# Four attention layers on 128 small graphs: graphs in pairs, three Strassen projections, leaky relu in PSUM, a planner by due times

## The chip, the cores and the metric

The kernel runs on one NeuronCore of a Trainium2 chip. The core has a matrix engine (TensorE, PE in the profile, with its weight loads as PEld), a vector engine (VectorE, DVE), an activation engine (ScalarE, ACT), a general engine (GpSimd, POOL), a queue engine that here issues nearly all transfers (SyncE, SP), and 16 DMA engines. Each engine works through its own list of instructions in order[...]. TensorE writes to PSUM[...]; GpSimd and DMA work on SBUF. The metric is the time of one execution on the device, in microseconds.

## The reference

128 graphs of 128 nodes with 512 features go through four attention layers. Each layer's result is added to its input and layer-normed.

```python
x = _layernorm(x + _L0_gnn_ref(x, adj, ...))   # scores from x itself, mixes x
x = _layernorm(x + _L1_gnn_ref(adj, x, ...))   # two GAT layers: 512 -> 4 heads x 256, elu, then 1024 -> 512, one head
x = _layernorm(x + _L2_gnn_ref(x, adj, ...))   # 8 heads of 64
x = _layernorm(x + _L3_gnn_ref(x, adj, ...))   # scores from 32 features, mixes x, elu
```

An attention is always the same: two numbers per node and head, their outer sum through a leaky relu with slope 0.2, a mask from the adjacency matrix, a softmax, and a product with the features:

```python
h = jnp.einsum('bnf,hfo->bhno', x, W)
e = jax.nn.leaky_relu(s1[..., :, None] + s2[..., None, :], negative_slope=ALPHA)
attn = jax.nn.softmax(jnp.where(mask, e, NEG_INF), axis=-1)
h_prime = jnp.einsum('bhnm,bhmo->bhno', attn, h)
```

There are 15 attention heads per graph: one, four, one (both parts of the second layer), eight and one. All arithmetic is f32.

## The kernel before

One graph is one stage of a software pipeline. A function `graph(g)` writes down the graph's operations as a list of `Op` objects, each with its engine, a cost in us, the buffers that it reads and writes, and a closure that emits it.

Order. `Pipeline.plan` places one graph's operations on a circle of 28 us (`PERIOD`), each engine's spans disjoint modulo the period, with a random shift from a fixed seed. `Pipeline.order` then takes all graphs' operations by those times and runs a list schedule over them, with 8 PSUM banks and a counted number of buffers for each size, and may take an operation up to 20 us (`AHEAD`) out of turn. The result is one fixed list per engine. The planner knows costs and latencies[...].

A graph's way. `first` loads x and adj, makes masks (`mask`, L738), two scores by a product with a running sum (`score`, L744), and calls `spread` and `attend`. `spread` (L580) brings a column of scores to every partition: a transpose on VectorE (L589), a transfer to a row in DRAM (L592), a transfer that broadcasts it (L596). `attend` (L637) has for each head of 128 x 128: the leaky relu on ScalarE from that broadcast with the own score as bias (L646, SBUF to SBUF), the mask with a running minimum on VectorE (L654, two SBUF inputs), the exponential with its sum on ScalarE (L663), and a reciprocal (L671). `turned` (L602) transposes through DRAM: 32x32 blocks on VectorE (L607), a transfer out (L612) and a transfer back in pieces (L622, or L617 where the result is a moving operand). `mixed` (L722) is the product, `resid` (L732) adds, `norm` (L678) is the layer norm: statistics on VectorE, a root on ScalarE (L685, L686), an offset on GpSimd (L692), the scaling on ScalarE (L699).

Three projections. The first (`project`, L704) multiplies x of one graph by `w1s` in 4 column blocks of 258 columns and 4 steps over the features: 16 matmuls per graph, each block in its own bank, copied out by ScalarE (L717). The second (`halves`, L749) takes two graphs together as a 2x2 block matrix and does Strassen's scheme (the variant of Winograd): 7 products instead of 8, of 4 matmuls with 257 columns each, 28 for a pair; sums of the left side on GpSimd (L780), partial results copied by ScalarE (L807) and added by VectorE (L812). The third (`project` again, with `wha`) has 2 blocks of 273 columns and 4 steps, 8 matmuls per graph.

`third` also holds the last layer: `scores` and `normed` do small arithmetic on two numbers per node on VectorE (L956 to L969). Each working buffer is a tile of its own; tiles of equal size share places.

SyncE issues 30 transfers per graph, 60 for two. The part of `attend` that matters most:

```python
nc.scalar.activation(z.ap[:, h, :], db.ap[:, h0 + h, :], AF.Prelu, bias=src(h0 + h), alpha=SLOPE)
nc.vector.tensor_tensor_reduce(
    out=zz.ap[:, h, :]..., in0=z.ap[:, h, :]..., in1=mask.ap..., scale=-1.0, scalar=FMAX,
    op0=ALU.add, op1=ALU.min, accum_out=nm.ap[:, h : h + 1])
```

Of the kernel before, what the change touches and what calls it, by code (L numbers as in the profile page):

```python
# [26 lines left out]

PERIOD = 28.0
LATENCY = {"PE": (0.0, 0.8), "DVE": (0.15, 1.44), "ACT": (0.1, 1.44), "POOL": (0.1, 1.44), "SP": (7.06, 7.06)}
FLOW = {"PE": (0.0, 0.6), "DVE": (0.15, 0.8), "ACT": (0.1, 0.8), "POOL": (0.1, 0.8), "SP": (4.5, 4.5)}
AHEAD = 20.0
URGENCY = 0.6
BANKS = 8

SEED, SPREAD = 989, 8.0


class Buf:


    def __init__(self, tag, shape, dtype=F32):
        self.tag, self.shape, self.dtype = tag, shape, dtype
        self.size = 1
        for d in shape[1:]:
            self.size *= d

        if dtype is F32 and shape[0] == P and self.size in (P, 4 * P, 8 * P) and not tag.startswith(("ps", "scr")):  # L50
            self.tag = f"w{self.size}"
        self.ap = self.slot = None

    def view(self, tl):
        if self.tag[0] == "w" and len(self.shape) > 2:
            dims = "abc"[: len(self.shape) - 1]
            tl = tl.rearrange(f"p ({' '.join(dims)}) -> p {' '.join(dims)}", **dict(zip(dims, self.shape[1:])))
        return tl


class Op:
    def __init__(self, engine, cost, emit, ins, outs, extra, uses=(), dma=0.0):
        self.dma = dma
        self.engine, self.cost, self.emit, self.extra = engine, cost, emit, extra
        self.wait = 0
        self.ins, self.outs = ins, outs
        self.uses = list(uses)
        self.bufs = list(dict.fromkeys([*ins, *outs, *uses]))

    def done(self, reader=None):  # L70
        own, other = LATENCY[self.engine]
        return self.cost + self.extra + (own if reader is self.engine else other)


class Pipeline:
    def __init__(self, make, n, place):
        self.make, self.n, self.place = make, n, place

    def plan(self, ops):


        before, after = [set() for _ in ops], [[] for _ in ops]
        last, readers = {}, {}
        for k, op in enumerate(ops):
            for b in op.ins:
                before[k].add(last[b])
            for b in op.outs:
                if b in last:
                    before[k].add(last[b])
                before[k].update(readers.get(b, ()))  # L90
            before[k].discard(k)
            for q in before[k]:
                after[q].append(k)
            for b in op.ins:
                readers.setdefault(b, set()).add(k)
            for b in op.outs:
                last[b], readers[b] = k, set()
        left = [0.0] * len(ops)
        for k in reversed(range(len(ops))):
            left[k] = ops[k].cost + max(  # L100
                (left[q] + ops[k].done(ops[q].engine) - ops[k].cost for q in after[k]), default=0.0
            )
        taken = {e: [] for e in LATENCY}
        times, ready, missing = [0.0] * len(ops), [0.0] * len(ops), [len(q) for q in before]
        waiting = [k for k in range(len(ops)) if not missing[k]]
        rng = random.Random(SEED)
        shift = [SPREAD * rng.random() for _ in ops]
        while waiting:
            k = min(waiting, key=lambda k: (ready[k] - URGENCY * left[k] + shift[k], k))
            waiting.remove(k)  # L110
            op, t = ops[k], ready[k]
            spans = taken[op.engine]
            while True:
                u = t % PERIOD
                clash = [
                    y + d - u for x, y in spans for d in (-PERIOD, 0.0, PERIOD)
                    if u < y + d - 1e-9 and x + d < u + op.cost - 1e-9
                ]
                if not clash:
                    break  # L120
                t += min(clash) + 1e-9
                assert t < ready[k] + 2 * PERIOD, "the period is too short"
            spans.append((t % PERIOD, t % PERIOD + op.cost))
            times[k] = t
            for q in after[k]:
                ready[q] = max(ready[q], t + op.done(ops[q].engine) + max(ops[q].wait, 0) * PERIOD)
                missing[q] -= 1
                if not missing[q]:
                    waiting.append(q)
        return times  # L130

    def run(self, setup):
        times, events = self.plan(self.make(None)), [(t, -1, k, op) for k, (t, op) in enumerate(setup)]
        for g in range(self.n):
            for k, op in enumerate(self.make(g)):
                if op is not None:
                    events.append((g * PERIOD + times[k], g, k, op))
        events.sort(key=lambda e: e[:3])
        for g, op in self.order(events):
            for b in op.outs:  # L140
                if b.ap is None and b.slot is not None:
                    b.ap = self.place(b, g)
            op.emit()

    def order(self, events):

        ops, n = [e[3] for e in events], len(events)
        ends, first, last, readers, open_uses = {}, {}, {}, {}, {}
        before, after = [0] * n, [[] for _ in ops]
        makes, coming = [[] for _ in ops], {}  # L150
        for i, op in enumerate(ops):
            need = {last[b] for b in op.ins + op.uses if b in last}
            for b in op.outs:
                need.update([last[b]] if b in last else [], readers.get(b, ()))
                if b not in first:
                    first[b] = events[i][0]
                    if b.tag != "const":
                        makes[i].append(b)
                        coming.setdefault(b.tag, []).append(i)
            need.discard(i)  # L160
            before[i] = len(need)
            for q in need:
                after[q].append(i)
            for b in op.ins + op.uses:
                readers.setdefault(b, []).append(i)
            for b in op.outs:
                last[b], readers[b] = i, []
            for b in op.bufs:
                open_uses[b] = open_uses.get(b, 0) + 1
                ends[b] = max(ends.get(b, 0.0), events[i][0] + op.done())  # L170

        free = {}
        for b, t in first.items():
            if b.tag != "const":
                places = free.setdefault(b.tag, [])
                s = next((s for s, e in enumerate(places) if e <= t), len(places))
                places[s : s + 1] = [ends[b]]
        assert len(free["ps"]) <= BANKS, "too few banks"
        free = {tag: [(0.0, s) for s in range(BANKS if tag == "ps" else len(p))] for tag, p in free.items()}
        ready, released, clock, lane = [0.0] * n, {}, {e: 0.0 for e in FLOW}, 0.0  # L180
        known = {e: [i for i in range(n) if not before[i] and ops[i].engine == e] for e in FLOW}
        issued, low, out = [False] * n, 0, []

        def start(i):
            t = max(clock[ops[i].engine], ready[i])
            for b in makes[i]:

                rank = 0
                for q in coming[b.tag]:
                    if q >= i or rank >= len(free[b.tag]):  # L190
                        break
                    rank += 1
                if rank >= len(free[b.tag]):
                    return None
                t = max(t, free[b.tag][rank][0])
            return t

        while len(out) < n:
            best = None
            for e, waiting in known.items():  # L200
                found = None
                for i in waiting:
                    if events[i][0] > events[low][0] + AHEAD and i != low:
                        break
                    t = start(i)
                    if t is not None and (found is None or t < found[0]):
                        found = (t, i)
                        if t <= clock[e]:
                            break
# [34 lines left out]
def tile_gat_stack(  # L244
# [63 lines left out]
    def mark():  # L308

        return Buf("const", [P, 1])  # L310
# [740 lines left out]
```

## Time and profile before

| what | us |
|---|---|
| median of 3 runs | 3246.22 (3245.11 to 3246.83) |
| span of the profiled execution | 3258.4 |
| first output leaves (from the span's start) | 355.1 |
| last input is loaded | 2996.0 |
| mean granted clock of TensorE | 0.976 of full |

The profile is of one execution, whose span is 12 us (0.4%) above the median of the runs. A row of the groups has the line, the engine, the operation, output and inputs, shapes and count, then the busy time together and the mean of one in ns, then the idle time of the engine just before these instructions and who ended it. A busy time is the time in which at least one instruction of the group ran, so where instructions overlap in the pipeline it is less than count times mean. DMA carries 606 MB with 1.66 million packets, 1.31 million of them under 512 bytes; the 16 DMA engines are busy 75% of the span.

### The profile page before, as it was taken

The page shows a single profiled execution, that of the slowest core. Times are in us where ns is not written, and L with a number is a line of the kernel's source. Part 1 is how long each engine was busy: PE and PEld are TensorE (multiplying, and loading weights), DVE is VectorE, ACT ScalarE, POOL GpSimd, SP SyncE. Part 2 cuts the span into 40 slices and gives each one's busy share as a digit, 9 for nine tenths or more (in the row PEclk, how much of TensorE's full clock was granted, in tenths as well). Part 3 has the DMA queues.
Part 4 walks back from the last instruction along what each step waited for, and adds up shares of the span by engine and source line. Part 5 has one row for each costly group of instructions (what it writes and reads, how often), then busy time and mean ns, then how long its engine had stood idle before and what let it go on. Part 6 is the DMA issues. An engine that isn't in the chain of part 4 may idle for free. (4 is left out here: it accounts for less than half of the span.)

```text
span 3258.4 us, 62058 instructions
## 1 busy us (share of the span) xinstructions
PE 3066.8 (94%) x14822; PEld 2488.7 (76%) x14822; DVE 2779.0 (85%) x9833; ACT 2451.2 (75%) x8741; POOL 1895.1 (58%) x2347
## 2 busy tenths in 40 slices
PE   6899999999999999999999999999999999999984
PEld 4688887787777877877777778777787777878853
DVE  4779888888888988898888889889898898989875
ACT  2457787787777777787777877777877777778875
POOL 4655655665565655665555665565566556565533
PEclk7899999999999999999999999999999999999985
DMA  4358777877877877877778777877787787777875
GB/s 119 94 136 196 183 205 188 200 193 190 203 187 188 205 186 192 201 190 200 188 187 200 191 188 204 189 190 201 191 204 187 188 205 188 196 196 190 197 174 129
DMA packets 1657567, 606.08 MB, mean 186 GB/s; under 512 B 1311562, under 2 KB 1508170, under 8 KB 1657204
## 3 DMA queue, kind: packets, MB, share of 16 engines
q1 hardware_dynamic: 1655836, 598.97, 75.0%
q8 instruction: 120, 1.97, 0.2%
q14 instruction: 243, 1.99, 0.2%
q0 software_dynamic: 576, 2.10, 0.2%
q10 hardware_dynamic: 792, 1.06, 0.1%
HBM read 374.43 MB, written 227.48 MB: 185 GB/s over the span
## 5 line engine op out<-in xcount | busy, mean ns | idle before, releaser
L710 PE MATMUL ps<-w1s,w 128*128 128x258 f32 x4096 | 926.9, 384 | 48.5 <-DMA w<-scr 25.0
L710 PEld LDWEIGHTS ps<-w1s,w 128*128 128x128 f32 x4096 | 777.0, 191 | 186.3 <-DVE xl L812 39.5
L654 DVE CUSTOM_DVE_ANT_0 w<-w,w 128x128 f32<-128x128 f32 x1920 | 861.1, 544 | 65.6 <-ACT w L646 49.2
L794 PE MATMUL ps<-w2s,w 128*128 128x257 f32 x3584 | 849.0, 383 | 8.5 <-POOL w L780 8.4
L663 ACT ACTIVATE w<-w,nm 128x128 f32<-128x128 f32 x1920 | 748.0, 394 | 98.2 <-DVE nm L654 76.3
L794 PEld LDWEIGHTS ps<-w2s,w 128*128 128x128 f32 x3584 | 669.1, 191 | 188.8 <-issue 80.0
L646 ACT ACTIVATE w<-w,xl 128x128 f32<-128x128 f32 x1536 | 488.8, 389 | 279.9 <-DMA w<-row 259.1
L607 DVE STREAM_TRANSPOSE w<-w 128x512 f32<-128x512 f32 (+1 forms) x1024 | 551.5, 540 | 34.3 <-ACT w L663 13.3
L710 PE MATMUL ps<-wha,w 128*128 128x273 f32 x2048 | 502.3, 398 | 7.3 <-DMA w<-scr 6.9
L710 PEld LDWEIGHTS ps<-wha,w 128*128 128x128 f32 x2048 | 383.2, 192 | 87.4 <-DVE w L607 6.3
L699 ACT ACTIVATE w<-w,mr,rd 128x512 f32<-128x512 f32 x512 | 415.2, 811 | 33.9 <-POOL mr L692 33.0
L692 POOL TENSOR_SCALAR mr<-mv,rd 128x1 f32<-128x1 f32 x512 | 160.1, 313 | 409.4 <-ACT rd L686 201.8
L663 ACT ACTIVATION_READ_ACCUMULATOR w<-w,nm 128x1 f32 x1920 | 368.1, 192 | 0.0
L681 DVE BATCH_NORM_STATS2 st<-w 128x6 f32<-128x512 f32 x512 | 337.2, 668 | 5.4 <-POOL w L986 4.6
L881 POOL TENSOR_TENSOR xl<-xl,b1t 128x512 f32<-128x512 f32 x256 | 335.2, 1310 | 1.6
L938 PEld LDWEIGHTS ps<-xl,w 128*128 128x128 f32 x2048 | 274.3, 196 | 80.8 <-issue 24.4
L646 ACT ACTIVATE w<-w,sc 128x128 f32<-128x128 f32 x384 | 152.3, 397 | 227.6 <-DMA w<-row 226.6
L725 PE MATMUL ps<-w,w 128*128 128x512 f32 x512 | 277.4, 624 | 32.6 <-DMA w<-scr 31.6
L738 POOL TENSOR_SCALAR w<-adj 128x128 f32<-128x128 int32 x256 | 192.4, 752 | 188.2 <-DMA adj<-in_adj_dram 75.1
L717 ACT COPY xl<-ps 128x258 f32<-128x258 f32 (+1 forms) x768 | 273.2, 362 | 31.8 <-PE ps L710 31.3
L938 PE MATMUL ps<-xl,w 128*128 128x66 f32 x2048 | 265.2, 273 | 27.7 <-DMA w<-scr 14.4
L654 DVE DVE_READ_ACCUMULATOR2_ANT nm<- 128x1 f32 x1920 | 290.5, 151 | 0.0
(213 smaller groups left out, 4258.8 us busy)
## 6 DMA issues: line engine op xcount, KB each, us to landing
scr<-w SPq DMA_DIRECT2D x640, 256.0 KB
w<-scr SPq DMA_DIRECT2D x640, 256.0 KB
w<-row SPq DMA_DIRECT2D x128, 512.0 KB
w<-in_x_dram SPq DMA_DIRECT2D x128, 256.0 KB
w<-row SPq DMA_DIRECT2D x128, 256.0 KB
out_dram<-w SPq DMA_DIRECT2D x128, 256.0 KB
w<-row SPq DMA_DIRECT2D x384, 64.0 KB
scr<-w SPq DMA_DIRECT2D x384, 64.0 KB
```

Of the source, the lines that this page charges most:

```text
L607: op("DVE", 0.12 + 0.133 * n, lambda: nc.vector.transpose(zb.ap.rearrange("p b h c -> p h b c"), src.ap.rearrange("p (h b c) -> p h b c", ...
L646: nc.scalar.activation(z.ap[:, h, :], db.ap[:, h0 + h, :], AF.Prelu, bias=src(h0 + h), alpha=SLOPE)
L654: nc.vector.tensor_tensor_reduce(out=zz.ap[:, h, :].rearrange("p (b a) -> p a b", b=4), in0=z.ap[:, h, :].rearrange("p (a b) -> p a b", b= ...
L663: nc.scalar.activation(zz.ap[:, h, :], zz.ap[:, h, :], AF.Exp, bias=nm.ap[:, h : h + 1], scale=-1.0, accum_out=rs.ap[:, h : h + 1],)
L681: op("DVE", 0.6, lambda: nc.vector.bn_stats(st.ap, y.ap), [y], [st])
L699: op("ACT", 0.7, lambda: nc.scalar.activation(y.ap, y.ap, AF.Identity, bias=mr.ap, scale=rd.ap), [y, rd, mr], [y])
L710: op("PE", w * 4 / 2400 + 0.006, lambda k=k: nc.tensor.matmul(px.ap[:, :w], lhsT=lhs.ap[:, k, :], rhs=wa(k, c), start=(k == 0), stop=(k == ...
L717: op("ACT", 0.06 + w / 1200, lambda: nc.scalar.copy(dst(), px.ap[:, :w]), [px], [t])
L725: op("PE", width * 4 / 2400, lambda: nc.tensor.matmul(pa.ap[:, :width] if len(xv.shape) == 2 else pa.ap.rearrange("p (s c) -> p s c", s=2) ...
L794: return lambda: nc.tensor.matmul(q[b].ap[:, :C2], lhsT=x()[:, k, :], rhs=w2s[:, slot, k, :], start=(fresh and k == 0), stop=(k == 3), ski ...
L881: op("POOL", 1.3, lambda nh=nh: nc.gpsimd.tensor_add(xl.ap[:, nh, : 2 * FH], xl.ap[:, nh, : 2 * FH], b1t[:, nh * 2 * FH : (nh + 1) * 2 * F ...
L938: op("PE", 0.225, lambda u=u, h=h: nc.tensor.matmul(pa.ap[:, u * CH : (u + 1) * CH], lhsT=pt.ap[:, u, :], rhs=xl3.ap[:, h * CH : (h + 1) * ...
```

## The change

Two graphs now are one unit of the pipeline, `pair(n)`; there are 64.

1. Transfers. `first` loads x and adj of both graphs with one transfer each, the output leaves with one, and `spread` and `turned` carry both graphs' data in one transfer where they can. SyncE issues 31 transfers per pair. The bytes are the same.
2. Projections. All three go through `strassen`, which takes the two graphs as a 2x2 block matrix. The first is done for each half of the columns: 2 x 7 products of 2 matmuls with 258 columns; the second 7 of 4 with 257; the third 7 of 2 with 273. `w1s` and the third weights (`w3s`, formerly `wha`) get three more combined blocks, made once by four subtractions on VectorE (`combined`). `sums` makes four sums of the left side on GpSimd for each projection. One product uses three banks; at most two products are open at once (`PRODUCTS`).
3. `attend` writes the leaky relu to a PSUM bank, from which the mask reads. Up to four heads share a bank.
4. `norm` handles both graphs' small numbers in one instruction each; the arithmetic of `scores` and `normed` on two numbers per node goes to GpSimd except for one reduction.
5. Order. `plan` walks one pair's operations from the end and gives each a due time: 1.28 (`STRETCH`) times the longest way before it. Pair n is due 44.5 us (`PACE`) after pair n-1. `lay_out` runs one list schedule over everything, by due times, up to 80 us ahead. It books [...]the time of DMA descriptors, and the parts of an operation, so that the second head's mask may follow the second head's relu. The setup's due times move forward, for the third weights from 70..134 to 45..77.
6. Memory. All working tiles of at least 64 f32 per partition are parts of one tile, `arena`, at places found from their lifetimes in that schedule.

```diff
-PERIOD = 28.0
-AHEAD = 20.0
-SEED, SPREAD = 989, 8.0
+STRETCH, PACE, AHEAD = 1.28, 44.5, 80.0
+SEED, SPREAD = 1, 0.0
+BANKS, PRODUCTS = 8, 2
+LOADS = 15.0
...
+    def combined(t, w, ready, engines):
...
+        sub(0, engines[0], 5, 2, 3, ready)
+        sub(1, engines[1], 3, 3, 0, [*ready, marks[0]])
+        sub(2, engines[2], 4, 2, 3, [marks[1]])
+        sub(3, engines[3], 6, 1, 4, [marks[2]])
+        return marks
...
-    w1s = const.tile([P, 4, 2, N1], F32, name="w1s")
+    w1s = const.tile([P, 7, 2, N1], F32, name="w1s")
...
     def attend(db, h0, nh, src, mask, scaled=False):
-            z, zz, nm, rs, ri = (Buf(f"{t}{nh}", s) for t, s in (
+        z = bank()
+        zz, nm, rs, ri = (Buf(f"{t}{nh}", s) for t, s in (
...
-                        z.ap[:, h, :], db.ap[:, h0 + h, :], AF.Prelu, bias=src(h0 + h), alpha=SLOPE
+                    z.ap[:, h * P : (h + 1) * P], db.ap[:, h0 + h, :], AF.Prelu, bias=src[1]()[:, h : h + 1], alpha=SLOPE
...
-            op("ACT", 0.08 + 0.293 * nh, prelu, [db, src.buf], [z])
-            op("DVE", 0.08 + 0.225 * nh, masked, [z, mask], [zz, nm])
-            op("ACT", 0.39 * nh, exp, [zz, nm], [zz, rs])
+        op("ACT", [0.4] * nh, prelu, [db, src[0]], [z])
+        op("DVE", [0.24] * nh, masked, [z, mask[0]], [zz, nm])
+        op("ACT", [0.387] * nh, exp, [zz, nm], [zz, rs])
...
+        def root():
+            nc.scalar.activation(rd.ap, mv.ap[:, :, 1], AF.Ln, bias=eps)
+            nc.scalar.activation(rd.ap, rd.ap, AF.Exp, scale=-0.5)
...
+    def sums(left, shape):
...
+        (a11, a12), (a21, a22) = left
+        summed(0, ALU.add, a21, a22)
+        summed(1, ALU.subtract, own[0], a11)
+        summed(2, ALU.subtract, a11, a21)
+        summed(3, ALU.subtract, a12, own[1])
...
+    def strassen(left, s, w, nk, wide, cols, to, out, ready):
+        pa, pb, pc = bank(), bank(), bank()
...
+        product(pa, left[0][0], 0, True)
...
+        taken(pa, t1)
+        product(pc, left[0][1], 1, True)
+        added(pc, t1, 0, 0)
+        product(pa, s[1], 4, False)
+        product(pb, s[0], 3, True)
+        taken(pa, u2)
+        taken(pb, v)
+        product(pa, s[2], 5, False)
+        product(pb, s[3], 2, False)
+        added(pa, v, 1, 1)
+        added(pb, u2, 0, 1)
+        product(pa, left[1][1], 6, False)
+        copied(pa, wide, lambda: to(1, 0), joins=[out[1]])
...
+        def normed():
+            nc.gpsimd.tensor_add(sc4.ap, sc4.ap, sz.ap)
+            nc.gpsimd.tensor_mul(sc4.ap, sc4.ap, rd.ap.unsqueeze(2).to_broadcast([P, 2, 2]))
+            nc.gpsimd.tensor_mul(sw.ap, swf.ap.unsqueeze(1).to_broadcast([P, 2, 2]), md.ap.unsqueeze(2).to_broadcast([P, 2, 2]))
+            nc.gpsimd.tensor_add(sc4.ap, sc4.ap, sw.ap)
...
+    for n in range(pairs):
+        begin = len(ops)
+        pair(n)
+        if offsets is None:
+            own = ops[begin:]
+            offsets = plan(own)
+        for o, t in zip(ops[begin:], offsets):
+            o.due = n * PACE + t
```

`taken` copies a bank to SBUF on ScalarE; `added` adds a bank and such a copy on VectorE; `product` is a chain of matmuls into a bank, where a last argument False adds to what the bank holds.

## The prediction

> **What bounds the kernel now.** I read the page's shares first, then the table by stages, then the groups of TensorE and VectorE in an undisturbed stretch, then the waits.
>
> ```profile
> PE 3066.8 (94%) x14822; PEld 2488.7 (76%) x14822; DVE 2779.0 (85%) x9833; ACT 2451.2 (75%) x8741; POOL 1895.1 (58%) x2347
> ...
> PE   6899999999999999999999999999999999999984
> ```
>
> TensorE is nearly full in all slices but the first two and the last. Stages (columns: PE, weight loads, DVE, ACT, POOL busy, each with its instructions, then the granted clock, the DMA share and GB/s):
>
> ```profile
> 0.00:100.00 100.00, 73.47 (x207) 45.56 (x208) 52.14 (x173) 30.91 (x90) 53.83 (x61) 0.80 0.42 112
> ...
> 1000.00:2000.00 1000.00, 964.13 (x4747) 788.44 (x4748) 876.91 (x3136) 782.74 (x2813) 597.29 (x741) 1.00 0.79 193
> ...
> 3100.00:3200.00 100.00, 77.63 (x300) 57.91 (x299) 76.98 (x299) 75.68 (x270) 34.36 (x56) 0.80 0.76 183
> ```
>
> ```profile
> L710 PE MATMUL ps<-w1s,w 128*128 128x258 f32 x1312 | 295.5, 383 | 18.2 <-DMA w<-scr 9.7 <-DVE st L681 3.1 <-DVE ri L671 3.0
> L794 PE MATMUL ps<-w2s,w 128*128 128x257 f32 x1170 | 276.2, 382 | 0.6 <-POOL w L780 0.6
> L710 PE MATMUL ps<-wha,w 128*128 128x273 f32 x656 | 158.0, 393 | 0.0
> ```
>
> These are the groups from 1000 to 2000 us. An f32 matmul leaves two records. A graph needs 16 matmuls of w1s, so 32 records, and 1312 records are 41.0 graphs in 1000 us: 24.39 us a graph, 48.78 us a pair. TensorE is busy 964.13/20.5 = 47.03 us of a pair and idle 1.75. So in steady state TensorE bounds. 128 graphs at 24.39 are 3122 us; filling and draining cost the other 136 us of the 3258.4. Per pair the others are busy: DVE 42.8, ACT 38.2, POOL 29.1 us, and DMA 0.79 x 48.78 = 38.5 us.
>
> Part of DVE's time is not work. Two engines at the same moment (start, duration):
>
> ```profile
> 1001.87 0.37 DVE L654 CUSTOM_DVE_ANT_0 w<-w,w 128x128 f32<-128x128 f32 x1
> ...
> 1002.09 1.50 DVE L654 CUSTOM_DVE_ANT_0 w<-w,w 128x128 f32<-128x128 f32 x1
> ```
>
> ```profile
> 1002.07 1.27 POOL L780 TENSOR_TENSOR w<-w,w 128x512 f32<-128x512 f32 x1
> ```
>
> The same masking instruction takes 0.37 us alone and 1.50 us when a GpSimd sum began 0.02 us earlier; it ends 0.25 us after that sum.
>
> ```profile
> L654 DVE CUSTOM_DVE_ANT_0 w<-w,w 128x128 f32<-128x128 f32 x620 | 274.6, 539 | 19.2 <-ACT w L646 12.5 <-DMA row<-w 5.3 <-ACT w L663 0.7
> ...
> L812 DVE TENSOR_TENSOR xl<-ps,u 128x257 f32<-128x257 f32 x81 | 32.6, 403 | 9.0 <-ACT u L807 8.9
> ...
> L959 DVE TENSOR_TENSOR sc<-sc,xl 128x2 f32<-128x2 f32 x41 | 26.6, 648 | 1.4
> ```
>
> Its mean is 539 ns; the line's own answer for 1000 to 1500 us gives a median of 383. L812, one input in PSUM, lies between 378 and 427 ns throughout. L959, two tiny inputs in SBUF, takes 648.
>
> [...]
>
> **The change, part by part, per pair of graphs.**
>
> TensorE. The first projection goes from 32 matmuls of 258 columns to 28, the third from 16 of 273 to 14. From the groups: 295.5/656 = 0.450 us and 158.0/328 = 0.482 us each, so 4 x 0.450 + 2 x 0.482 = 2.77 us. The groups overlap: all of TensorE's groups add to 1036 us against 964 busy, so I take 0.93 of it, 2.6 us. The second projection keeps its 28, the attention products keep count and shape. Busy 47.0 - 2.6 = 44.4 us.
>
> DVE. 30 masks lose the lock: 30 x (0.539 - 0.383) = -4.7. [...] I take +1.0. Strassen additions go from 4 to 12: 8 x 0.403 = +3.2. The last layer's score arithmetic (L959, L966, L969: 648, 240, 236 ns) goes to GpSimd: -2.25. Merged single-head transposes, spreads, reciprocals and m1: about -1.8. Sum 42.8 - 4.55 = 38.3.
>
> ACT. Copies out of PSUM stay at 16. Layer-norm roots halve: 4 x (0.286 + 0.203) = -2.0. The 30 leaky relus into PSUM: the diff books 0.4 us each, before it booked 0.293, so up to +3.2[...]. I take +1.5. Sum 37.7.
>
> POOL. Eight new sums of 256 elements, at half of L780's 1.288 us: +5.2. Score arithmetic +1.4; paired masks -1.2, offsets and others -0.8. Sum 33.7.
>
> DMA. The bytes stay. The pieces of 128 bytes stay too, except in the last layer's and the second layer's transposes, which get twice as long; 37.5 to 38.5 us. SP issues 31 transfers a pair in place of 60. SP is in order, but its waits are on data and it isn't what TensorE waits for: TensorE's own waits on a transfer are 18 us in 1000.
>
> So TensorE still leads with 44.4, then DVE 38.3, DMA 38, ACT 37.7. Nothing hides the saving on TensorE itself: it is on the engine that sets the pace. The merges elsewhere are worth nothing directly; they are cover. If that cover fails, DVE is next.
>
> Order. The new planner replaces both the modulo plan and the list. Its quality can't be read from before. What stays idle now:
>
> ```profile
> PEld ps L710 <- DVE xl L812: 18.0, 13, 2.1
> ```
>
> Half of TensorE's 36 idle us in 1000 stand behind the last addition of a Strassen product. For the cost of new products the bounds are: no idle at all (the 28 matmuls of L794 waited 0.6 us for anything), or 12 new turnarounds, each with a cover of two matmuls (0.9 us) in place of four (1.9). I keep the 1.75 us a pair[...]. Pace 44.4 + 1.75 = 46.15 us, 64 pairs 2954 us.
>
> Fill and drain, 136 us now. The added subtractions on w1s (four like L495's 1.23 us) and on w3s lie in the fill, about +7 us; a pair has twice the work at each step of the tail, +13. Loads and products of the third weights come some 60 us earlier in their due times, which could give 25 back. Bounds 110 to 200, taken 156. The arena adds no instruction. It would cost if two tiles in it waited for each other without need; exponentials that start after their own head's mask (ACT at 1023.69, while masks run until 1025.1) show that waits go by parts of a tile.
>
> Sum against the profiled execution: 2954 + 156 = 3110 us span. The median, 3246.22, lies 12 us below that execution's span; so 3098, rounded to 3095.
>
> **The rivals.**
> - A, the forecast, 3095.
> - B, a better order: without lock stalls the plan holds, idle halves to 0.9 and fill is 140: 64 x 45.3 + 140 - 12 = 3027. For it: half of the present idle time is one repeated wait. Against: ACT and POOL get fuller.
> - C, the relu in PSUM doesn't free DVE: guarded by bank, the first mask must wait until the last of four relus has left the bank. Up to 3 x 0.3 us for six groups of four and 0.3 for three of two is 6.3 us; DVE then has 44.6 us, as much as TensorE. Two full engines in fixed order: 47.9 us a pair, 64 x 47.9 + 156 - 12 = 3210. Against it: the mask can be placed later in DVE's order.
> - D, slower: the turnaround. Strassen reuses bank pa after ACT has copied it, and ACT is in order, with bursts of four relus or exponentials (1.25 to 1.5 us). Twelve new turnarounds of 0.9 us cover lose x each; from x = 0.19 us, 48.5 us a pair, all gain is gone. At x = 0.3: 64 x 49.75 + 156 - 12 = 3328. For it: the wait above, 0.22 us for each turnaround of today if all of it is counted so. Against: L794 itself hardly waits, and two products may be interleaved.
>
> **How the numbers follow.** Chances: A 0.48, B 0.18, C 0.17, D 0.15, no change 0.02. The range 2985 to 3230 takes in A, C and nearly all of B with the bounds of fill and relu; D is left out. A alone spans 3040 to 3150. No change means within 0.2%, 6.5 us, about what such a measurement can tell: faster 0.83, same 0.02, slower 0.15.
>
> **What would show it.** In the profile after: 28 w1 matmuls a pair and TensorE near 44.4 us busy and 96% full in the middle stages; masks with mean near median (below 0.42 us); DVE near 83%. Wrong if DVE waits before the masks for relus by several us a pair (C), if TensorE waits for ACT's copies inside a product (D), if the relu is far above 0.4 us, or if the pace is good but the tail longer than 200 us.

## The result and the profile after

The kernel after takes 4006.91 us (median of four runs, 4001.64 to 4013.14); the kernel before, run beside it, 3246.52 us (3245.11 to 3252.51). The ratio is 1.233, with a 95% interval of 1.230 to 1.237: slower by 23%, where 4.7% faster was forecast. The profiled execution of after has a span of 3999.9 us.

The page of after, its shares and two of its slice rows:

```profile
PE 3216.1 (80%) x14054; PEld 2479.8 (62%) x14054; DVE 2576.1 (64%) x9269; ACT 2466.6 (62%) x8229; POOL 2212.4 (55%) x2859
...
PE   6688878888888888887888888888888888888873
...
PEclk8899898999989999989999999998999999988986
```

The instruction counts are those of the change: 14054 instead of 14822 records on TensorE, 9269 instead of 9833 on VectorE. The work was removed as planned, and VectorE is busy for 203 us less. Yet TensorE, the busiest engine, is down from 94% to 80%, and its whole middle is evenly slow: 8 (twice 7) in nearly every slice where before had a 9. So the loss lies neither at the start nor at the end.

The same stages as before (PE, weight loads, DVE, ACT, POOL busy, then granted clock, DMA share, GB/s):

```profile
600.00:2600.00 2000.00, 1656.99 (x7310) 1277.75 (x7309) 1319.95 (x4803) 1281.06 (x4293) 1145.54 (x1483) 0.92 0.70 157
1000.00:2000.00 1000.00, 831.17 (x3661) 640.73 (x3660) 661.49 (x2410) 641.67 (x2133) 577.37 (x742) 0.92 0.71 158
```

The pace is read from the start times of the matmuls of w1s and w2s: a straight line through those of the middle pairs (10 to 57) rises by 59.48 us a pair here and by 48.44 before. (Counting matmuls in a stretch, as the forecast did, can be off by one burst of them, about 1%.) Over 64 pairs that is 64 x 11.04 = 707 us of the 741.5 us between the two spans. A stretch of 2000 us holds 33.6 pairs. VectorE's work per pair is 1319.95/33.6 = 39.3 us, ScalarE's 38.1, GpSimd's 34.1, all within about 1 us of the forecast's 38.3, 37.7 and 33.7. The engines do what was foreseen and stand still in between. What they wait for, over the whole run (engine, line, released by: us in total, times, longest):

```profile
POOL arena L734 <- DMA row<-arena: 513.3, 135, 12.0
ACT arena L702 <- DMA row<-arena: 375.4, 165, 6.5
ACT arena L719 <- DMA row<-arena: 356.5, 65, 7.1
POOL arena L864 <- DMA row<-arena: 346.3, 59, 7.7
...
PEld ps L711 <- DVE arena L756: 287.3, 135, 6.2
DVE arena L756 <- DMA row<-arena: 272.7, 101, 4.5
DVE arena L620 <- DMA row<-arena: 264.5, 68, 6.0
PE ps L711 <- DVE arena L756: 220.2, 91, 5.8
```

Three engines wait for one and the same kind of transfer, and at lines that have nothing to do with it: L734 adds blocks for a Strassen product, L719 copies a bank, L702 normalises. `row<-arena` writes one row of 128 numbers per head to DRAM (1 to 8 KB in all), from the small tile `sT`. Nobody but the next transfer needs its result. SyncE, which issues it, waits as well:

```profile
SPq L602 <- DMA arena<-scr: 506.3, 220, 8.2
SPq L602 <- DMA arena<-row: 339.8, 159, 5.4
```

L602 is this transfer's issue. Its data come from VectorE; here it waits for other transfers *into* the arena that it doesn't read. The timeline shows one such moment (start, duration; idle before and its releaser in brackets):

```profile
1997.05 0.30 DVE L686 BATCH_NORM_AGGREGATE mv<-st 128x2 f32<-128x6 f32 x2
2000.20 0.54 SPq L602 DMA_DIRECT2D row<-arena  x1
2001.82 0.38 ACT L719 COPY arena<-ps 128x258 f32<-128x258 f32 x1 [7.10 <-DMA row<-arena]
...
2001.89 0.76 DVE L756 TENSOR_TENSOR arena<-ps,arena 128x258 f32<-128x258 f32 x2 [4.55 <-DMA row<-arena]
2001.96 1.53 POOL L734 TENSOR_TENSOR arena<-arena 128x256 f32<-128x256 f32 x2 [4.33 <-DMA row<-arena]
...
2002.71 0.80 PE L711 MATMUL ps<-w1s,arena 128*128 128x258 f32 x1 [4.39 <-DVE arena L756]
```

The transfer is issued at 2000.20. Within 0.14 us of each other, from 2001.82, ScalarE, VectorE and GpSimd start again after 7.1, 4.6 and 4.3 us of nothing, and TensorE 0.8 us later, behind VectorE's addition. The table by stages, in steps of 2 us (columns as above), shows the same moment from all engines:

```profile
1996.00:1998.00 2.00, 2.00 (x11) 1.69 (x9) 0.95 (x4) 0.00 (x0) 1.63 (x2) 1.00 1.03 108
1998.00:2000.00 2.00, 0.32 (x2) 0.00 (x0) 0.00 (x0) 0.00 (x0) 0.00 (x0) 1.00 0.09 10
2000.00:2002.00 2.00, 0.00 (x0) 0.00 (x0) 0.11 (x1) 0.18 (x1) 0.04 (x1) 1.00 0.00 1
2002.00:2004.00 2.00, 1.29 (x3) 1.10 (x4) 1.87 (x5) 2.00 (x11) 1.92 (x3) 0.63 0.18 52
2004.00:2006.00 2.00, 2.00 (x6) 1.54 (x6) 1.49 (x4) 2.00 (x13) 0.87 (x2) 0.52 0.04 14
```

From 1998.3, where TensorE's last matmul ends, to 2001.8 next to nothing runs, the DMA engines included; afterwards TensorE's clock (third number from the end) is at 0.52 to 0.63. It looks like a barrier: all earlier writers of the arena must have ended before the transfer starts, and no later writer may begin before it ends. The built programs, which list what each instruction waits for, fit that. First after, then the same kernel with `sT` in a tile of its own:

```
L602 DMACopy row_65_10691<-arena 4x2x32 [waits DMAHW2,DMAHW1,DMAHW3,DVE,DMAHW4,Activation,Pool]
L602 DMACopy row_65_10799<-sT_65_10791 4x2x32 [waits DVE]
```

In the first it waits for the ends of transfers, by four semaphores (DMAHW), and for VectorE, ScalarE and GpSimd; in the second for VectorE alone.

The theory: `in_=sT.ap[0:P:32]` reads partitions 0, 32, 64, 96. Inside a shared tile, the tracking of dependencies takes a read with a stride over partitions as a read of the whole tile, while slices of columns are told apart. There are five such transfers a pair. In the waits of the whole run engines stand behind `row<-arena` for some 2560 us, and for 8 us behind `scr<-arena`, the transfers that read column slices over all partitions out of the same tile. The rivals: the arena as such (waits between its columns), the new order or the Strassen turnarounds (D).

### The profile page after: what moved, and what is told of

The parts are those of the page before. It is cut to its first block, busy times and chain, and to the rows that moved or that the text cites. A ratio compares the mean times of both kernels' runs of the same rounds, so it can differ in the third digit from the quotient of the medians.

```text
span 3999.9 us, 56735 instructions
## 1 busy us (share of the span) xinstructions
PE 3216.1 (80%) x14054; PEld 2479.8 (62%) x14054; DVE 2576.1 (64%) x9269; ACT 2466.6 (62%) x8229; POOL 2212.4 (55%) x2859
## 3 DMA queue, kind: packets, MB, share of 16 engines
q14 instruction: 214, 1.75, 0.2%
## 5 line engine op out<-in xcount | busy, mean ns | idle before, releaser
L711 PE MATMUL ps<-w1s,arena 128*128 128x258 f32 x3584 | 1003.1, 432 | 369.1 <-DVE arena L756 188.9
L711 PEld LDWEIGHTS ps<-w1s,arena 128*128 128x128 f32 x3584 | 742.7, 214 | 653.3 <-DVE arena L756 220.1
L734 POOL TENSOR_TENSOR arena<-arena 128x256 f32<-128x256 f32 (+1 forms) x768 | 706.4, 934 | 711.8 <-DMA row<-arena 513.3
L711 PE MATMUL ps<-w2s,arena 128*128 128x257 f32 x3584 | 889.1, 402 | 101.1 <-DVE arena L880 56.9
L711 PEld LDWEIGHTS ps<-w2s,arena 128*128 128x128 f32 x3584 | 711.7, 201 | 295.3 <-DVE arena L880 93.1
L663 ACT ACTIVATE arena<-arena,nm 128x128 f32<-128x128 f32 x1920 | 741.4, 390 | 69.0 <-DVE nm L654 68.4
L719 ACT COPY arena<-ps 128x258 f32<-128x258 f32 (+2 forms) x1024 | 352.0, 377 | 694.0 <-DMA row<-arena 356.5
L620 DVE STREAM_TRANSPOSE arena<-arena 128x512 f32<-128x512 f32 (+1 forms) x832 | 527.8, 639 | 375.9 <-DMA row<-arena 264.5
L702 ACT ACTIVATE arena<-arena,mr,rd 128x512 f32<-128x512 f32 x512 | 408.8, 815 | 510.3 <-DMA row<-arena 375.4
L711 PE MATMUL ps<-w3s,arena 128*128 128x273 f32 x1792 | 538.7, 441 | 185.7 <-ACT arena L719 118.1
L654 DVE CUSTOM_DVE_ANT_0 arena<-ps,arena 128x128 f32<-128x128 f32 x1920 | 527.8, 378 | 115.0 <-ACT ps L647 86.2
L647 ACT ACTIVATE ps<-arena 128x128 f32<-128x128 f32 x1536 | 567.9, 371 | 43.4 <-DMA arena<-row 3.6
```

What stands on the lines that cost most here:

```text
L620: op("DVE", 0.075 + 0.134 * m, lambda a=a, src=src: nc.vector.transpose(zb.ap[:, :, a * m : (a + 1) * m, :].rearrange("p b h c -> p h b c" ...
L647: nc.scalar.activation(z.ap[:, h * P : (h + 1) * P], db.ap[:, h0 + h, :], AF.Prelu, bias=src[1]()[:, h : h + 1], alpha=SLOPE)
L654: nc.vector.tensor_tensor_reduce(out=zz.ap[:, h, :].rearrange("p (b a) -> p a b", b=4), in0=z.ap[:, h * P : (h + 1) * P].rearrange("p (a b ...
L663: nc.scalar.activation(zz.ap[:, h, :], zz.ap[:, h, :], AF.Exp, bias=nm.ap[:, h : h + 1], scale=-1.0, accum_out=rs.ap[:, h : h + 1],)
L702: op("ACT", 0.715, lambda g=g, y=y: nc.scalar.activation(y(), y(), AF.Identity, bias=mr.ap[:, g : g + 1], scale=rd.ap[:, g : g + 1]), [b, ...
L711: nc.tensor.matmul(px.ap[:, :w], lhsT=lhs(k), rhs=rhs(k), start=(fresh and k == 0), stop=(k == nk - 1), skip_group_check=True,)
```

## The experiments

In the first group before took 3226.1 us (3220.9 to 3233.25), in the second 3221.7 (3215.77 to 3229.14). Paces are read from start times as above, busy times a pair from 600 to 2600 us.

**One tile taken out of the arena.** Everything else of the change stays.

```diff
-        self.arena = shape[0] == P and self.size >= 64 and tag not in ("ps", "const") and not tag.startswith("scr")
+        self.arena = ... and not tag.startswith(("scr", "sT"))
```

> The changed kernel, with one thing altered: the small tiles sT, from which SyncE sends the rows of scores to DRAM, lie outside the arena. Theory F (the row transfer, which reads every 32nd partition of the one arena tile, counts as reading all of the arena, so it waits for all earlier writers and all later writers wait for it): the waits on the row transfer vanish on ACT, DVE and POOL (together some 2400 us now), a pair takes 46 to 48.5 us in place of 59.6, the span is 3080 to 3260. Theory T (turnaround inside Strassen products, TensorE waiting for L756 and L719) leaves the waits of TensorE for those lines near their 650 us and the time above 3600.

Measured: 3070.16 us (3068.21 to 3071.91), ratio to before 0.952 [0.950, 0.954]. The barrier and all of the loss are gone, and this version beats both kernels. Its page and middle stages:

```profile
PE 2877.5 (94%) x14054; PEld 2348.2 (76%) x14054; DVE 2587.1 (84%) x9269; ACT 2445.2 (80%) x8229; POOL 2208.9 (72%) x2859
```

```profile
600.00:2600.00 2000.00, 1961.92 (x9754) 1614.40 (x9754) 1776.71 (x6409) 1696.00 (x5729) 1525.02 (x1972) 1.00 0.93 210
```

That is 44.6 us a pair, a little less than the 46 to 48.5 expected. TensorE is busy 43.8 us a pair and idle 0.85. The counts are those of after to the instruction, so the 930 us between the two are waiting and a lower clock (0.908 granted over the whole execution, against 0.974), not work.

**The arena alone, in the kernel before.** Its order, its projections and its masks stay; its working tiles, `sT` among them, become parts of one tile.

```diff
+    def lies_in(b):
+        return b.slot is not None and b.shape[0] == P and b.size >= 32 and b.tag not in ("ps", "const") and not b.tag.startswith("scr") ...
...
     def place(b, g):
+        if lies_in(b):
+            a = at_place[b.tag, b.slot]
+            tl = arena[0][:, a : a + b.size]
```

> The kernel before, its order of instructions unchanged, but all working tiles (the sT too) laid into one arena tile. Theory F: five row transfers a graph become meeting points of ACT, DVE, POOL and SyncE; 10 for two graphs where the changed kernel has 5, so at least as bad as it: above 3900 us, perhaps 4500. If pairs, Strassen or the new order made the loss, an arena alone does nothing: 3247 within 1%.

Measured: 4643.18 us, ratio 1.440 [1.437, 1.443], 70.7 us a pair. Nothing of the change but the arena was in it. The two longest waits:

```profile
POOL arena L698 <- DMA row<-arena: 1142.2, 222, 8.6
DVE arena L632 <- DMA row<-arena: 949.0, 250, 9.3
```

**The same arena, `sT` outside.**

```diff
-        return b.slot is not None and ... and not b.tag.startswith("scr")
+        return b.slot is not None and ... and not b.tag.startswith("scr") and not b.first_tag.startswith("sT")
```

The `sT` of the four-head attention, which in before lies in a place that it shares with other tiles of its size, gets two tiles of its own here.

> The kernel before with the same arena, but the sT tiles outside. Theory F: nothing left to wait for without need: 3247 us within 1%. If an arena costs by itself (releases, false waits of other transfers): near the run with everything in the arena.

Measured: 3220.32 us, ratio 0.998 [0.997, 0.999], 47.7 us a pair. So an arena costs nothing where no strided read lies in it, and the rival "the arena as such" falls. The new order isn't needed for the loss either.

**Same place, same bytes, another form of the read.** In after, with `sT` in the arena, the transfer is issued as four, of one partition each.

```diff
-            out=row.ap.rearrange("h (b c) -> b h c", b=P // 32), in_=sT.ap[0:P:32]
+            to = row.ap.rearrange("h (b c) -> b h c", b=P // 32)
+            for i in range(P // 32):
+                nc.sync.dma_start(out=to[i : i + 1], in_=sT.ap[32 * i : 32 * i + 1])
```

> The changed kernel with sT left in the arena, but each row transfer (partitions 0, 32, 64, 96) split into four transfers of one partition each. Theory F, in its narrow form (the stride over partitions makes the footprint too wide, not the arena): the wide waits vanish though sT is in the arena; 20 transfers a pair in place of 5 cost SyncE about 8 us a pair[...], so 3150 to 3500 us. If any read of the arena by a transfer counts as reading all of it: no better than the changed kernel, 4000 or more.

Measured: 3242.41 us, ratio 1.005 [1.003, 1.007], 47.4 us a pair. Two of the three longest waits are now these:

```profile
DVE arena L657 <- ACT ps L650: 373.3, 295, 4.9
...
ACT ps L650 <- DMA arena<-row: 248.4, 95, 5.1
```

ScalarE no longer waits for `row<-arena` at all, VectorE for 4.6 us and GpSimd for 19.5 us in the whole run, although the same cells of the arena are read. So it is the stride inside the shared tile that makes the barrier, not the place of `sT` alone. Twenty transfers a pair in place of five cost 2.8 us of pace against the version with `sT` outside. ScalarE's wait for the spread rows (last line) is 49.4 us in all with `sT` outside, so their later arrival is what shows of that cost.

**Three of five.** `sT` of the three single-head attentions goes back into the arena; the others stay outside.

```diff
-        self.arena = ... and not tag.startswith(("scr", "sT"))
+        self.arena = ... and not tag.startswith(("scr", "sT4", "sT8", "sT16"))
```

> As e1_st_out, but the sT tiles of the three single-head attentions of a pair lie in the arena again, those of the two attentions with more heads stay outside: 3 of the 5 row transfers of a pair are wide. Now 5 cost 59.6 - 45.45 = 14.15 us a pair, 2.8 us each. If each wide transfer costs by itself: 45.45 + 8.5 = 54 us a pair, 64 pairs and 161 us for the ends, 3610 us span, 1.12 times the kernel before. If a few such meeting points are enough to set the pace: near the changed kernel, 1.2. If they hide behind each other: under 1.05.

Measured: 3729.58 us, ratio 1.159 [1.157, 1.161], 54.9 us a pair: (54.9 - 44.6)/3 = 3.4 us for each barrier. All five make (59.5 - 44.6)/5 = 3.0, the ten of the arena in before (70.7 - 47.7)/10 = 2.3. So the loss grows with the number of such reads, at 2.3 to 3.4 us each, somewhat more for the three than the 2.8 expected. The price of one is lower where there are more, but the three cases also differ in which attentions and which order they have, so that this is not shown to come from the number.

With the barrier explained, the next runs ask what the rest of the change is worth; they all have `sT` outside.

**First projection without Strassen**: 32 matmuls a pair again, no combined weights.

```diff
-        s = sums(left, [P, 2, P])
-        for j in range(2):
-            cols = slice(j * C1, (j + 1) * C1)
-            strassen(left, s, w1s, 2, C1, cols, lambda g, h, cols=cols: xl[g].ap[:, h, cols], xl, w1_ready)
+        for g in G:
+            project(part(xT, slice(4 * g, 4 * g + 4)), ...)
```

> As e1_st_out, but the first projection without Strassen: 32 matmuls a pair in place of 28, no sums, no additions for it. If TensorE's work sets the pace and turnarounds cost nothing: 4 x 0.447 = 1.8 us a pair more, 3180 us, 3.5% above e1_st_out. If the turnarounds of Strassen cost as much as rival D had it (0.19 us for each of the 8 that go): no gain or loss against e1_st_out within 1%.

Measured: 3110.88 us, ratio 0.966 [0.965, 0.968], 45.3 us a pair: 1.3% above the version with `sT` outside, between the two outcomes that were expected.

```profile
1000.00:2000.00 1000.00, 998.53 (x4992) 830.62 (x4992) 807.79 (x3023) 833.89 (x2834) 679.60 (x884) 1.00 0.84 208
```

TensorE is busy 99.9% of the time, 45.2 us a pair and idle 0.07. With Strassen it is 43.8 and idle 0.85. The four matmuls save 1.4 us, and 0.8 of that comes back as idle time; 0.6 a pair stays, 40 us over 64 pairs, which is all of the 40.7 us between the two. Where TensorE idles is in its groups from 600 to 2600 us, first with Strassen on the first projection, then without:

```profile
L711 PE MATMUL ps<-w1s,arena 128*128 128x258 f32 x2509 | 560.4, 380 | 0.0
L711 PE MATMUL ps<-w3s,arena 128*128 128x273 f32 x1248 | 327.5, 396 | 31.2 <-ACT arena L719 30.0 <-issue 1.2
```

```profile
L710 PE MATMUL ps<-w3s,arena 128*128 128x273 f32 x1244 | 318.9, 393 | 0.0
```

The products of the first projection wait for nothing. The gaps stand in the third, whose scheme is the same in both versions, and close when the first has more matmuls. So part of a saving on the bounding engine was given back as gaps on that same engine, but not by the turnarounds of the products that made the saving. Why the third waits only then was not tested.

**Leaky relu back in SBUF**, in place in the broadcast tile; the planner again keeps the mask apart from GpSimd's work. The control is the version with `sT` outside at the same `SLACK` of 1.0 (a margin of the planner for the lifetimes of tiles); it takes 3068.47 us, so `SLACK` itself does nothing.

```diff
-                    z.ap[:, h * P : (h + 1) * P], db.ap[:, h0 + h, :], AF.Prelu, ...
+                    db.ap[:, h0 + h, :], db.ap[:, h0 + h, :], AF.Prelu, ...
...
-                    in0=z.ap[:, h * P : (h + 1) * P].rearrange("p (a b) -> p a b", b=4),
+                    in0=db.ap[:, h0 + h, :].rearrange("p (a b) -> p a b", b=4),
```

> The control for relu_sbuf: e1_st_out with tiles in the arena reused 1 us after their planned end in place of 2. Same order of instructions; within 0.5% of e1_st_out.

> As e1_slack1, but the leaky relu written in place into the broadcast tile in SBUF, so that the mask has two SBUF inputs again. The lock comes back: mean of the mask from 0.382 to about 0.54 us, 30 masks a pair, 4.7 us more of VectorE, which has 40.3 of 45.45 now; as TensorE leads, +0 to +4% against e1_slack1. If the waits for a bank shared by four relus (2.9 us a pair in front of the masks) and the longer relu in PSUM cost more than the lock, it is faster than e1_slack1.

Measured: 3233.65 us, ratio to before 1.004 [1.002, 1.005], 5.4% above the control and so above the 4% expected at most, 47.6 us a pair. The stage and the masks:

```profile
1000.00:2000.00 1000.00, 939.87 (x4584) 766.69 (x4583) 947.06 (x3007) 774.52 (x2695) 709.42 (x925) 0.98 0.88 197
```

```profile
L654 DVE CUSTOM_DVE_ANT_0 arena<-arena 128x128 f32<-128x128 f32 x631 | 306.4, 598 | 1.5 <-ACT arena L647 1.1
```

And the masks of the version with the relu in PSUM, in the same stretch:

```profile
L647 ACT ACTIVATE ps<-arena 128x128 f32<-128x128 f32 x536 | 197.3, 371 | 30.1 <-DMA arena<-row 17.1
...
L654 DVE CUSTOM_DVE_ANT_0 arena<-ps,arena 128x128 f32<-128x128 f32 x670 | 185.8, 382 | 64.8 <-ACT ps L647 64.7
```

A mask takes 598 ns instead of 382, which is 30 x 0.216 = 6.5 us a pair, and VectorE, at 94.7%, is now slightly busier than TensorE. The trace of before shows what comes back with two inputs in SBUF, the forecast's lock: its 692 masks that overlap a TENSOR_TENSOR of GpSimd by more than 0.05 us take 839 ns on average, the other 1228 take 378. In after, with one input in PSUM, 1343 masks overlap one and take 378 on average, 402 at most. From 600 to 2600 us VectorE is busy 45.1 us a pair, with the relu in PSUM 39.7. In this version, whose order was planned anew with the same `PACE`, fewer products, merged transfers and the new planner together gain nothing.

## Why the prediction was wrong

**The step that failed** is one sentence: "The arena adds no instruction. It would cost if two tiles in it waited for each other without need; exponentials that start after their own head's mask ... show that waits go by parts of a tile." The observation was right for what it saw, slices of columns. It was carried over to every access, and one access of the kernel, L602, reads by another pattern. Before, the same read with the same stride was harmless, because it covered a small tile: only the size of the tile around it changed. The trace of before showed `row<-sT` with waits almost only for VectorE (506 of 519 us at its issue, L592); the question to ask of each transfer out of the arena, what it would wait for if it held the whole of it, was not asked. The cost was put at nothing, and no rival had it; the slower rival, D, was a different mechanism. The 1.75 us of idle time a pair that the forecast kept became 59.5 less TensorE's 49.3 us (1656.99/33.6), about 10 us. Of the 14.8 us a pair that the five barriers cost against the version with `sT` outside, 9.3 are idle time of TensorE and 5.5 are the same matmuls taking longer, at a granted clock of 0.92 in place of 1.00 (from 600 to 2600 us a record of w1s takes 427 ns on average in place of 380).

**The rest of the sum** can be read from the version with `sT` outside, which is the change as the forecast understood it. It took 0.952 of before; the forecast's 3095 is 0.953 of 3246. That closeness is partly luck, since two terms miss in opposite directions:
- The saving on TensorE was put at 2.6 us a pair, and is 46.8 - 43.8 = 3.0.
- Idle time kept at 1.75, the author's estimate, is 0.85. So the pace is 44.6 and not 46.15: 97 us less over 64 pairs.
- Fill and drain, taken as 156, are 3070 - 64 x 44.64 = 213 us: 57 more, above even the bound of 200. By the same working before has 3258 - 64 x 48.44 = 158 us, so the change adds 55. (The forecast's 48.78 and 136 for before came from a count of matmuls, one too high and the other too low by the same 22 us.) Strassen on the first projection, with its combined weights, makes 3 of it (213 against 210 without); the rest wasn't taken apart.
- VectorE 39.7 (38.3 forecast), ScalarE 37.9 (37.7), GpSimd 34.0 (33.7). The lock on the masks went as foreseen: their mean is 382 ns, and in after, with the same masks, the longest of 1920 takes 402, where before it was 1522. Reading PSUM added nothing: the median there is 380 ns against 382 before, in place of the +1.0 us taken for it, which was the author's estimate. Other terms of VectorE are therefore some 2.4 us larger. One is a small addition with two inputs in SBUF (L900), 1124 ns on average from 1000 to 2000 us where its two forerunners (L915) took 221 each, 0.7 us a pair; the rest stays open.
- ScalarE's relu: 197.3/536 = 0.368 us of busy time each into PSUM, against 156.6/492 = 0.318 into SBUF before, so +1.5 us for 30, the value taken.
- DMA was put at 37.5 to 38.5 us a pair and is 0.93 x 44.6 = 41.5, for the same bytes in fewer packets. Without Strassen on the first projection, with the same transfers, it is 0.84 x 45.3 = 38.1.

**The rivals.** C's mechanism is there: in after four relus run from 2024.31 to 2025.90 us and the first of their masks begins at 2025.93. With `sT` outside VectorE waits 64.7 us in 1000 before masks for the relu, 2.9 us a pair of the 6.3 at most, but with 39.7 us of work it has room for them, so it doesn't bind. D's turnaround is small. The wait for ScalarE's copy inside the products of the version with `sT` outside, from 1000 to 2000 us:

```profile
PE ps L711 <- ACT arena L719: 15.4, 22, 0.7
```

That is 15.4/22.4 = 0.7 us a pair, 0.06 for each of 12 turnarounds on average, below the 0.19 at which D would decide; all of it falls on the third projection. Yet of the 19.5 us that TensorE is still idle in this stretch, four fifths are this wait.

**A line that was misread.** The forecast laid half of TensorE's 36 idle us to the last addition of a Strassen product, by the line `PEld ps L710 <- DVE xl L812: 18.0`. That line is of the weight loads, which run beside matmuls (788.44 us busy in the 1000 in which matmuls are for 964.13). The waits of the matmuls themselves in the same 1000 us of before:

```profile
PE ps L710 <- DMA w<-scr: 9.7, 9, 1.7
PE ps L725 <- DMA w<-scr: 8.7, 13, 1.2
...
PE ps L710 <- DVE xl L812: 0.3, 1, 0.3
```

Half of the idle time stood behind the transfers that bring transposed tiles back, and 0.3 us behind that addition. So B's idle time of 0.9 came true by luck, since its reason was the misread line, and D lost what spoke for it. With `sT` outside no matmul waits for such a transfer from 1000 to 2000 us.

**Where the forecast reasoned too narrowly** beside the arena: "The merges elsewhere are worth nothing directly; they are cover." That holds for the merges, but the relu in PSUM counted there only as a smaller VectorE share. Taken out, it costs 5.4%, more than Strassen on the first projection (1.3%), because VectorE's cover against the *new* pace of 44.6 is only 5 us and the lock is 6.5.

## What to carry to other kernels

When tiles are joined into a larger one, list every access of the parts by its pattern, above all those that skip partitions, and ask which waits each gets if it is taken as touching the whole: a transfer of 1 to 8 KB became a barrier of three engines here, some 3 us each time. Look for it in the waits as one transfer that releases engines at lines with no use for its data. And price a cover against the pace that the change is to reach, not against the present one.

## What was unexpected of the hardware

- Idle time of TensorE was paid twice. In the barrier above the granted clock is 1.00 before, and 0.63 and 0.52 in the 4 us after a pause of 4.39 us; the 6 matmuls of w1s there take 4.46 us, where 6 x 0.450 = 2.7 us would be usual. Some 10 us later a pause of 2.63 us was followed by the same: from 2016 to 2020 the clock is 0.54 and 0.60. Over 600 to 2600 us, busy share and clock are 0.98 and 1.00 with `sT` outside, 0.86 and 0.95 with three barriers a pair, 0.83 and 0.92 with five, 0.77 and 0.86 with the ten in before.
- A single relu takes 371 ns into PSUM and took 389 into SBUF. But consecutive ones into SBUF overlapped and those into PSUM hardly do (0.318 and 0.368 us busy each), so a row of four is slower into PSUM: 1.59 us in after (at 2024.31), 1.27 before (at 1018.42).
- Fewer packets didn't make the DMA engines less busy. With the same 606 MB, the main queue's packets took 75.0% of 3258.4 us before, 2444 us for 1.66 million, and 86.4% of 3070.1 with `sT` outside, 2653 us for 1.50 million. The version without Strassen on the first projection, with the same transfers, has a DMA share of 0.84 from 600 to 2600 us where the version with `sT` outside has 0.93, at nearly the same rate (207 and 210 GB/s). So the added time doesn't come from merging the transfers. What it comes from (wider w1s and so other places of the tiles, the order) was not tested.
